# Four changes of order in a local-attention and whitening kernel: a late sum in image 0, an early weight load, band transposes behind a softmax, late bias additions

## The chip, the cores and the metric

The kernel runs on one core of one Trainium2 chip. The time is the device time of one execution in microseconds, and lower is better. Five engines work side by side, each through its own list of instructions in order: PE (TensorE, the matmuls), DVE (VectorE), ACT (ScalarE), POOL (GpSimd) and SP (SyncE, which here only starts DMA transfers). They wait for each other by semaphores.

## What is computed

The input x has 4 images of 256 channels and 64 x 64 points, in fp32. Layer 0 computes, for every point, 49 weights from a 7 x 7 convolution with dilation 2 followed by a 1 x 1 convolution, makes them a softmax, and takes the weighted sum of the 49 neighbours at distance 2. Layer 1 whitens the result: it centres the channels, takes the covariance in 4 groups of 64 channels, finds the inverse root by 5 Newton steps and applies it, with a gain and a shift.

```python
k = conv(x, w1, padding=6, dilation=2) + b1          # 256 -> 128 channels, 7 x 7
k = conv(k, w2) + b2                                 # 128 -> 49, 1 x 1
attn = softmax(k, axis=1)
shifts = [x moved by (2u-6, 2v-6) for u in 0..6 for v in 0..6]
y = sum over k of shifts[k] * attn[k]
Sigma = 1e-5 * I + xc @ xc.T / m                     # xc: y less its mean, per group
P = I; 5 times: P = 1.5 * P - 0.5 * (P @ P @ P) @ (Sigma / trace)
out = (P * sqrt(1 / trace)) @ xc * gain + shift
```

## The kernel before

**Tiles and stages.** The two convolutions are folded into one of 49 outputs. An image is cut into two planes (even and odd rows of the picture); slot tiles hold them. The convolution is a Toom-Cook (Winograd) scheme in rows and columns: seven row points `br` (0 to 5 and `INF`), and under each of them seven column points in three banks (`BANKS`, line 26): points 1, 2, 0, then 3, 4, INF, then 5. For a row point, DVE and ACT combine the rows of x (`row_eval`), then the columns (`col_eval`, into the tiles `xh`), and the tap weights (`weights`, into the tiles `wr`). PE multiplies (`conv_bank`, line 536), ACT brings each bank's sums from PSUM to the tile `pv` (line 546), and DVE turns the points back (`col_interp` into the tile `zz`, then `row_interp` into the logits). `add`, `sub` and `madd` (lines 306, 309 and 313) are the helpers through which nearly all of the DVE arithmetic goes.

**Image 0 is special.** Its row points 0, 4, 5 and INF are convolved directly with the plane (`direct`, line 676), in two sums each for 0, 4 and 5: a first of 8 rows of points, which ACT copies to `zz` (line 688), and a second, whose last row ACT copies (line 690), and whose other rows DVE adds to `zz` (`add` at line 691). The direct sums lie in the PSUM tile `acc` or in a convolution bank. The part of the program for image 0 is run under `strict[0] = True`: `in_turn` chains each `add`, `sub` and `madd` to the one before it, so that DVE executes them in the order in which they are written.

**Images 1 to 3** run through all six of `ROWS` (0 to 5) and `direct_inf`. `conv_step(k, i)` issues bank i of row point k, then prepares bank i of the next row point, and after the last bank turns the columns back. The first time a pair of row point and bank is used, `weights` computes its weights and stores them in DRAM (`gd`, line 434); later images load them (line 378). For row points 4, 5 and INF, the row-combined weights are first read from DRAM (`kept`) into the tile `rb[0]` (line 387), and DVE and POOL read them there. For row point 5 of image 1 this load waits until DVE has read row point 4's weights, since they lie in the same tile.

**Between these steps** lies the attention of the previous image. `softmax` transposes logits with PE, takes maxima with DVE (line 865), exponentials with ACT (line 873) and scales with DVE (line 886). It runs twice for an image (`pc` 0 and 1). `move_terms` copies terms to the tile `zt` with ACT (line 919) and stores them to DRAM (`sd`, line 932); `load_band` reads them back in three parts as diagonals (`band`, line 960, four transfers to a part) and DVE transposes each part in blocks (line 973, under high priority). PE then transposes blocks of x (line 991), multiplies them with the band (`weighted_sum`, line 1020), ACT stores y with the pivot added (line 1039), PE transposes y (line 1052), ACT copies it (line 1060), and PE sums the moments (line 1073). The program's number n counts these units, four to an image: even n use the terms of softmax `pc` 0, odd n those of `pc` 1. The first band is that of n = 0.

**What sets the order.** Outside image 0 a scheduler orders each engine's list by the written order, priorities (`tc.high_priority`) and its own estimates of time; PE's order is written (`pe`). `later` is a list of small ACT steps that `conv_bank` releases behind the ACT copy of the next bank with i = 1: each entry is issued then and made to follow that copy (lines 550 to 560). Before the change only `col_interp`'s last copy (line 633) uses it. `row_interp(b, 0)` for images 1 to 3 is called after row point 4's last bank; it writes the first two of four phases of the logits, and two ACT instructions add the bias to them (line 658, in place). SP's list holds all its transfers in order, and each of them may also wait for the transfer that used the same completion semaphore before it.

Of the kernel before, what the change touches and what calls it, by code (L numbers as in the profile page):

```python
# [10 lines left out]
AF = mybir.ActivationFunctionType  # L11
# [21 lines left out]
def kernel(  # L33
# [330 lines left out]
    def weights(b, br, i, mid=None):  # L364

        first = (br, i) not in made  # L370
        made.add((br, i))
        s0 = slot_of[BANKS[i][0]]
        ns = sum(len(taps(bc)) for bc in BANKS[i])
        nk = NSK * len(taps(br)) // 2
        wt = apool.tile([P, ns, NSK], F32, tag=f"wr{i}", name=f"wr_{b}_{br}_{i}")[:, :, :nk]
        w = {bc: wt[:, slot_of[bc] - s0 : slot_of[bc] - s0 + len(taps(bc))] for bc in BANKS[i]}
        if not first:
            nc.sync.dma_start(wt, gd[br][:, s0 : s0 + ns])
            return w

        if br == 0:
            g = [gr0[:, v] for v in range(KS)]
        elif br in kept:

            f = rb[0].rearrange("p q r c w -> p (q r c w)")[:, : KS * nk]
            if i == 0:
                nc.sync.dma_start(f, kept[br])
            f = f.rearrange("p (v a r k) -> p v a r k", v=KS, a=NCC, k=KT)
            g = [f[:, v] for v in range(KS)]
        else:  # L390
            g = [gbr[:, v] for v in range(KS)]
        g = [t.rearrange("p a r k -> p (a r k)") for t in g]

        e = ct.rearrange("p a b -> p (a b)") if b else store[4].rearrange("p c r w -> p (c r w)")
        e, o, e1 = (e[:, k * nk : (k + 1) * nk] for k in range(3))
        g0 = [g[KS - 1 - a] for a in range(4)]
        g1 = [g[KS - 5 - a] for a in range(3)]
        o0 = {bc: w[bc][:, 0] for bc in w}
        o1 = {bc: w[bc][:, 1] for bc in w if bc != INF}

        same = nc.scalar.copy if b == 0 else nc.gpsimd.tensor_copy
        if i == 0:
            add(e, g0[0], g0[2])
            add(o, g0[1], g0[3])
            add(e1, g1[0], g1[2])
            add(o0[1], e, o)
            sub(o0[2], e, o)
            add(o1[1], e1, g1[1])
            sub(o1[2], e1, g1[1])
            same(o0[0], g0[0])  # L410
            same(o1[0], g1[0])
        elif i == 1:
            madd(e, g0[2], 4.0, g0[0])
            madd(o, g0[3], 4.0, g0[1])
            madd(e1, g1[2], 4.0, g1[0])
            madd(o0[3], o, 2.0, e)
            madd(o0[4], o, -2.0, e)
            madd(o1[3], g1[1], 2.0, e1)
            madd(o1[4], g1[1], -2.0, e1)
            same(o0[INF], g0[3])  # L420
        else:
            madd(o0[5], g0[0], 2.0, g0[1])
            madd(o1[5], g1[0], 4.0, g1[2])
            madd(o0[5], o0[5], 2.0, g0[2])
            if mid is not None:
                mid()
            madd(o1[5], g1[1], 2.0, o1[5])
            madd(o0[5], o0[5], 2.0, g0[3])
            add(o1[5], o1[5], o1[5])
        for bc in BANKS[i]:  # L430
            f = SCALE[bc] * (SCALE[br] if br not in kept else 1.0)
            if f != 1.0:
                nc.scalar.mul(w[bc], w[bc], f)
        nc.sync.dma_start(gd[br][:, s0 : s0 + ns], wt)
        return w
# [205 lines left out]
    def row_interp(b, part):  # L641

        pt = {k: zz[:K2, k] for k in range(NP)}
        lg = lgx
        if b == 0:
            lg = store[4].rearrange("p c r w -> p (c r w)")
        lg = lg[:, : SH * W].rearrange("p (r w) -> p r w", w=W)
        outs = phases(lg[:K2])
        cut = lambda t, k: t[:, k : k + Q8]
        tr = ct.rearrange("p a b -> p (a b)")[:K2, : Q9 * W].rearrange("p (q w) -> p q w", w=W)  # L650
        interpolate(pt, tr, outs, cut, part)
        if part == 0:
            done_ = ((0, outs[0]), (2, outs[2]))
        else:
            done_ = ((3, cut(pt[5], 0)), (1, outs[1]))
            logits[b] = lg
        for a, t in done_:
            nc.scalar.activation(outs[a], t, AF.Identity, bias=bias[:K2])

    logits = {}  # L660

    def direct(b, br, s, ps, w, xr=None):


        a = 3 if br == INF else 0
        order = [(v, cc) for v in sorted(range(KS), key=lambda v: abs(v - R)) for cc in range(NCC)]
        for j, (v, cc) in enumerate(order):
            d = 2 * (v - R)
            w0, w1_ = max(0, -d), min(W, W - d)
            for h in range(2):  # L670
                if xr is None:
                    xs = slots[2 * b + h].rearrange("p c (q a) w -> p a q c w", a=4)[:, a]
                else:
                    xs = xr[:, :, h]
                pe(
                    nc.tensor.matmul(  # L676
                        ps[h * HB : h * HB + KT, :, w0:w1_],
                        w[v][:, cc],
                        xs[:, :, cc, w0 + d : w1_ + d],
                        start=(j == 0),  # L680
                        stop=(j == len(order) - 1),
                        skip_group_check=True,
                    )
                )
        z = zz[:K2, br]
        if s == 0:
            with tc.high_priority():
                nc.scalar.copy(z[:, :Q8], ps[:K2])
        else:
            nc.scalar.copy(z[:, Q8], ps[:K2, Q8 - 1])  # L690
            add(z[:, 1:Q8], z[:, 1:Q8], ps[:K2, : Q8 - 1])

    def conv_psum():
        ncv[0] += 1
# [102 lines left out]
    for i in three:  # L797
        bank(2, i)
    row_weights(4)
    keep_weights(4)  # L800
    xrs[4] = row_eval(0, 4)
    direct0(4, 0)
# [46 lines left out]
    def softmax(b, pc):  # L849

        lv = logits[b].rearrange("p r w -> p (r w)")
        nm = f"{b}_{pc}"
        mx = work.tile([P, NCH, 2], F32, tag="mx", name=f"mx_{nm}")
        lt = []
        for hf in range(2):
            lt.append(tp().rearrange("p (i h k) -> p i h k", i=NI, h=2))
            for i in range(NI):
                pe(
                    nc.tensor.transpose(
                        lt[hf][:, i].rearrange("p h k -> p (h k)")[:, :K2],  # L860
                        lv[:K2, bass.ds(2 * (NI * hf + i) * P + pc, P, 2)],
                        ident[:K2, :K2],
                    )
                )
            nc.vector.tensor_reduce(
                mx[:, NI * hf : NI * (hf + 1)], lt[hf][:, :, :, :KT], AX.X, ALU.max
            )
        nc.vector.tensor_scalar(mx, mx, -1.0, None, ALU.mult)  # L868
        d = terms[b, pc] = bpool.tile([P, 2, NCH, KT], F32, tag="d", name=f"d_{nm}", bufs=2)
        s = work.tile([P, 2, NCH], F32, tag="s", name=f"s_{nm}")  # L870
        for h in range(2):
            for i in range(NCH):
                nc.scalar.activation(  # L873
                    d[:, h, i], lt[i // NI][:, i % NI, h, :KT], AF.Exp,
                    bias=mx[:, i, h : h + 1], accum_out=s[:, h, i : i + 1],
                )
            nc.vector.reciprocal(s[:, h], s[:, h])
            rm = work.tile([P, NCH, KS], F32, tag="rm", name=f"rm_{nm}_{h}")
            nc.vector.tensor_tensor(
                rm,  # L880
                s[:, h].unsqueeze(2).to_broadcast([P, NCH, KS]),
                cmask.unsqueeze(1).to_broadcast([P, NCH, KS]),
                ALU.mult,
            )
            dh = d[:, h].rearrange("p i (u v) -> p i u v", u=KS)
            nc.vector.tensor_tensor(
                dh, dh, rm.unsqueeze(2).to_broadcast([P, NCH, KS, KS]), ALU.mult
            )

    terms, moved, loaded = {}, set(), set()  # L890

# [57 lines left out]

    BAND = ((0, 3), (3, 5), (5, 8))  # L950

    def load_band(n, part):

        if (n, part) in loaded or n not in moved:
# [4 lines left out]
        for g in range(CR):  # L959
# [6 lines left out]
                ),  # L966
            )

        f = band.rearrange("p m r w -> p (m r) w")[
            :, m0 * BP + (R if m0 == 0 else 0) : m1 * BP - (R if m1 == NCH else 0)  # L970
        ].rearrange("p e w -> p (e w)")
        with tc.high_priority():
            nc.vector.transpose(f, f)  # L973
        if (n, part) == (4 * B - 1, len(BAND) - 1):
            bring_back(dma)

# [199 lines left out]

    def soft(b, pc):
        with tc.high_priority() if pc == 0 else nullcontext():
            softmax(b, pc)
        soft_done.add((b, pc))  # L1180
        if pc == 0:
            bands(4 * b)
# [263 lines left out]
```

## Time and profile before

| what | value |
|---|---|
| time, median of 3 runs | 752.98 us (752.46 to 753.97) |
| the profiled execution's own time | 753.07 us |
| its span, first to last instruction | 751.3 us |
| mean granted TensorE clock | 0.984 |
| PE busy | 706.7 us |
| DVE busy | 611.5 us |
| ACT busy | 332.3 us |

A page of the profile shows one execution. "Idle before" an instruction is the time that its engine stood still just before it, with what ended that wait behind an arrow. The timeline view lists instructions as start, length, engine, line, operation and tiles, and puts the idle time and its releaser in square brackets. "Granted clock" is the share of its full clock that PE had. The 1.8 us between the profiled execution's time and its span lie around the program.

### The profile page before, as it was taken

What the parts mean: (1) busy time and instruction counts of PE and PEld (TensorE: products, weight loads), DVE (VectorE), ACT (ScalarE), POOL (GpSimd) and SP (SyncE); (2) the same over time, 40 slices, a digit from 0 to 9 for tenths busy, and PEclk for the clock granted to TensorE, in tenths of its full rate; (3) what the DMA queues carried; (4) which work ended last, traced back from release to release, by engine and by line L of the source; (5) the groups of instructions that cost most, each with busy time, mean ns of one, the idle gap of its engine ahead of it and who ended that gap; (6) DMA issues with size and microseconds to landing.
All of it is one profiled execution on the core that took longest, in us unless ns stands there. A gap on an engine that the chain in (4) does not pass through costs nothing.

```text
span 751.3 us, 18491 instructions
## 1 busy us (share of the span) xinstructions
PE 706.7 (94%) x7512; PEld 531.5 (71%) x7512; DVE 611.5 (81%) x1268; ACT 332.3 (44%) x953; POOL 50.9 (7%) x52
## 2 busy tenths in 40 slices
PE   6999999997988997999999999999999889998996
PEld 1449643376887795599998976899998678885331
DVE  3799899998999988877997799799969665545575
ACT  1424240253564354375453443745435573322564
POOL 0410070020000110001000100000000000000000
PEclk9999999999999998999999999999999999999999
DMA  8981120127153393046743930433532243362588
GB/s 322 257 302 73 60 88 17 64 98 232 64 183 120 103 342 97 21 132 217 256 130 116 336 82 1 146 111 110 166 90 82 50 135 111 117 251 118 209 359 327
DMA packets 59629, 114.41 MB, mean 152 GB/s; under 512 B 22887, under 2 KB 42008, under 8 KB 58776
## 3 DMA queue, kind: packets, MB, share of 16 engines
q1 hardware_dynamic: 55848, 94.36, 37.7%
q0 software_dynamic: 3696, 18.88, 7.3%
q8 instruction: 59, 0.97, 0.5%
q14 instruction: 26, 0.21, 0.1%
HBM read 65.88 MB, written 47.33 MB: 151 GB/s over the span
## 4 chain that ended last, share of the span: by engine, by line
PE 60%; DVE 27%; ACT 5%; DMA 4%; issue 3%; SPq 1%; DVEq 0%; ACTq 0%
PE cv L536 18%; PE y L1020 13%; PE acc L676 6%; PE tp L1386 4%; PE sig L1073 3%; PE tp L1052 3%; PE cv L676 3%; PE tp L991 3%; DVE xh L313 3%; DVE pv L313 2%; DVE rb L313 2%; DVE zz L313 2%; DMA band<-sd 2%; DVE band L973 2%; PE cv L222 2%
## 5 line engine op out<-in xcount | busy, mean ns | idle before, releaser
L536 PE MATMUL cv<-xh,wr 128*49 128x128 f32 x4368 | 249.7, 275 | 5.9 <-DVE xh L306 5.6
L536 PEld LDWEIGHTS cv<-xh,wr 128*49 128x49 f32 x4368 | 243.6, 124 | 9.9 <-issue 7.1
L1020 PE MATMUL y<-band,xb 128*128 128x224 f32 (+2 forms) x640 | 154.6, 381 | 8.7 <-ACT xb L999 6.7
L1020 PEld LDWEIGHTS y<-band,xb 128*128 128x128 f32 x640 | 111.4, 196 | 31.4 <-ACT xb L999 9.4
L546 ACT COPY pv<-cv 113x486 f32<-113x486 f32 (+1 forms) x63 | 30.0, 476 | 84.6 <-PE cv L536 84.4
L1039 ACT ACTIVATE slot<-y,pivot 128x512 f32<-128x512 f32 x53 | 36.7, 740 | 67.5 <-PE y L1020 67.4
L1060 ACT COPY yt<-tp 128x256 f32<-128x256 f32 x128 | 45.5, 379 | 37.8 <-PE tp L1052 36.4
L973 DVE STREAM_TRANSPOSE band<-band 128x864 f32<-128x864 f32 (+1 forms) x48 | 47.6, 992 | 13.2 <-DMA band<-sd 13.1
L991 PE MATMUL tp<-ident,slot 128*128 128x128 f32 x256 | 50.0, 297 | 8.2 <-ACT yt L1060 8.2
L313 DVE SCALAR_TENSOR_TENSOR pv<-pv 113x162 f32<-113x162 f32 x186 | 55.2, 320 | 0.8 <-ACT pv L546 0.3
L1052 PE MATMUL tp<-ident,slot 128*128 128x128 f32 x256 | 52.0, 299 | 3.7 <-ACT yt L1060 1.0
L1052 PEld LDWEIGHTS tp<-ident,slot 128*128 128x128 f32 x256 | 41.2, 205 | 13.8 <-issue 4.0
L991 PEld LDWEIGHTS tp<-ident,slot 128*128 128x128 f32 x256 | 40.1, 205 | 14.8 <-ACT yt L1060 9.7
L873 ACT ACTIVATE d<-tp,mx 128x49 f32<-128x49 f32 x128 | 36.9, 337 | 21.4 <-DVE mx L868 17.9
L919 ACT COPY zt<-d 32x112 f32<-32x112 f32 (+2 forms) x156 | 44.8, 287 | 1.9
L313 DVE SCALAR_TENSOR_TENSOR xh<-ct 128x512 f32<-128x512 f32 x42 | 27.9, 685 | 13.7 <-PE cv L536 13.4
L1073 PEld LDWEIGHTS sig<-yt 128*64 128x64 f32 x1024 | 33.2, 140 | 6.4 <-issue 4.9
L1073 PE MATMUL sig<-yt 128*64 128x65 f32 x1024 | 37.7, 228 | 0.0
L999 ACT COPY xb<-tp 128x256 f32<-128x256 f32 x87 | 30.5, 375 | 14.0 <-PE tp L991 13.4
L999 DVE COPY xb<-tp 128x256 f32<-128x256 f32 x41 | 16.4, 421 | 23.4 <-PE tp L991 23.4
L676 PE MATMUL acc<-slot,tap 128*49 128x496 f32 (+3 forms) x168 | 34.6, 569 | 0.0
L873 ACT ACTIVATION_READ_ACCUMULATOR d<-tp,mx 128x1 f32 x128 | 30.8, 242 | 0.0
(222 smaller groups left out, 958.0 us busy)
## 6 DMA issues: line engine op xcount, KB each, us to landing
out_dram<-out SPq DMA_DIRECT2D x32, 512.0 KB, 3.4
sd<-zt SPq DMA_DIRECT2D x16, 896.0 KB, 4.0
slot<-in_x_dram POOLq DMA_DIRECT2D x12, 1024.0 KB, 10.1
band<-sd SPq DMA_DIRECT2D x128, 84.0 KB, 2.1
wr<-gd SPq DMA_DIRECT2D x15, 588.0 KB, 3.7
wr<-gd SPq DMA_DIRECT2D x15, 490.0 KB, 4.0
spill<-slot POOLq DMA_DIRECT2D x3, 2048.0 KB, 7.7
back<-spill SPq DMA_DIRECT2D x3, 2048.0 KB, 13.1
```

Of the source, the lines that this page charges most:

```text
L313: return in_turn(STT(o, a, f, b, ALU.mult, ALU.add))
L536: nc.tensor.matmul(cv[h * HB : h * HB + KT, k, sr : sr + n, sc : sc + n], wv[:, sc, sr, cc], xh[bc][:, :n, h * NCC + cc, :n], start=(j == ...
L676: nc.tensor.matmul(ps[h * HB : h * HB + KT, :, w0:w1_], w[v][:, cc], xs[:, :, cc, w0 + d : w1_ + d], start=(j == 0), stop=(j == len(order) ...
L873: nc.scalar.activation(d[:, h, i], lt[i // NI][:, i % NI, h, :KT], AF.Exp, bias=mx[:, i, h : h + 1], accum_out=s[:, h, i : i + 1],)
L919: ins = nc.scalar.copy(o, i)
L973: nc.vector.transpose(f, f)
L991: nc.tensor.transpose(t[:, cc * P : (cc + 1) * P], xt[:, cc, CR * m : CR * (m + 1), bass.ds(pc, SW, 2)], ident,)
L999: (nc.vector.tensor_copy if tail else nc.scalar.copy)(xb, t[:, :C])
L1020: nc.tensor.matmul(ps[:, cc, q0 - half * HALF : q1 - half * HALF, :], xb[:, cc * P : (cc + 1) * P], rhs, start=(k == 0), stop=(k == len(PI ...
L1052: nc.tensor.transpose(t[:, cc * P : (cc + 1) * P], yt[:, cc, CR * i : CR * (i + 1), bass.ds(pc, SW, 2)], ident,)
L1060: nc.scalar.copy(yb.rearrange("p a g c -> p (a g) c")[:, :, :GW], t[:, :C].rearrange("p (e c) -> p e c", c=GW),)
L1073: nc.tensor.matmul(sig[g * GW : (g + 1) * GW, cc], yb[:, cc, g, :GW], yb[:, cc, g], start=(count[0] == 0 and cc == 0), stop=(count[0] == 4 ...
```

## The change

The change touches four places.

1. In image 0 the second part of row point 0 (the ACT copy of the last row and the DVE `add` at line 691) is not issued inside `direct`, but put in the list `seconds`, and issued after `row_weights(4)`.
2. For row point 5 the row-combined weights are loaded into `lgx` and not into `rb[0]`. `lgx` is the tile in which the logits of images 1 to 3 are built; in image 1 they are first written after row point 5's weights were computed.
3. The three block transposes of the first band (n = 0) are not issued in `load_band`, but held, and issued after the second softmax of image 0, each made to follow that softmax's last DVE multiplication.
4. The two bias additions of `row_interp(b, 0)` for images 1 to 3 go through `later`, so that they follow the ACT copy of bank 1 of row point 5.

```diff
@@ weights
-            f = rb[0].rearrange("p q r c w -> p (q r c w)")[:, : KS * nk]
+            f = lgx if br == 5 else rb[0].rearrange("p q r c w -> p (q r c w)")
+            f = f[:, : KS * nk]
@@ row_interp
         for a, t in done_:
-            nc.scalar.activation(outs[a], t, AF.Identity, bias=bias[:K2])
+            def end(a=a, t=t):
+                return nc.scalar.activation(outs[a], t, AF.Identity, bias=bias[:K2])
+            if b > 0 and part == 0:
+                later.append(end)
+            else:
+                end()
@@ direct
-            nc.scalar.copy(z[:, Q8], ps[:K2, Q8 - 1])
-            add(z[:, 1:Q8], z[:, 1:Q8], ps[:K2, : Q8 - 1])
+            def second():
+                nc.scalar.copy(z[:, Q8], ps[:K2, Q8 - 1])
+                add(z[:, 1:Q8], z[:, 1:Q8], ps[:K2, : Q8 - 1])
+            if br == 0:
+                seconds.append(second)
+            else:
+                second()
+    seconds = []
@@ image 0
     row_weights(4)
+    seconds.pop()()
     keep_weights(4)
@@ softmax
-            nc.vector.tensor_tensor(
+            last = nc.vector.tensor_tensor(
                 dh, dh, rm.unsqueeze(2).to_broadcast([P, NCH, KS, KS]), ALU.mult
             )
+        return last
+    held = []
+    def release_held(after):
+        for f in held:
+            tc.add_manual_dep(
+                f().ins,
+                after.ins.name,
+                mybir.DependencyInfo(mybir.DependencyClass.NoSync, mybir.DependencyReason.DATA),
+                reason="release_held",
+            )
+        held.clear()
@@ load_band
-        f = band.rearrange("p m r w -> p (m r) w")[
-            :, m0 * BP + (R if m0 == 0 else 0) : m1 * BP - (R if m1 == NCH else 0)
-        ].rearrange("p e w -> p (e w)")
-        with tc.high_priority():
-            nc.vector.transpose(f, f)
+        def turn_blocks():
+            f = band.rearrange("p m r w -> p (m r) w")[
+                :, m0 * BP + (R if m0 == 0 else 0) : m1 * BP - (R if m1 == NCH else 0)
+            ].rearrange("p e w -> p (e w)")
+            with tc.high_priority():
+                return nc.vector.transpose(f, f)
+        if n == 0:
+            held.append(turn_blocks)
+        else:
+            turn_blocks()
@@ soft
         with tc.high_priority() if pc == 0 else nullcontext():
-            softmax(b, pc)
+            last = softmax(b, pc)
+        if pc == 1:
+            release_held(last)
```

## The prediction, as it was put on record

> **What bounds the kernel now.** I read the page's shares, then the list of waits of PE alone, then the timeline around each long wait.
>
> ```profile
> PE 706.7 (94%) x7512; PEld 531.5 (71%) x7512; DVE 611.5 (81%) x1268; ACT 332.3 (44%) x953; POOL 50.9 (7%) x52
> ```
>
> PE is busy for all but 751.3 - 706.7 = 44.6 us of the span. The order of PE's instructions is the same in both builds (I compared their lists), so a gain can come only from PE's idle time and from PE's clock.
>
> ```profile
> PE tp L991 <- ACT yt L1060: 8.2, 8, 3.8
> PE y L1020 <- ACT xb L999: 6.7, 12, 2.2
> PE cv L536 <- DVE xh L306: 5.6, 1, 5.6
> ```
>
> The columns are total, times, longest. A single wait of 5.6 us is on DVE; the ACT waits are traced one step further below. In time order they are (single lines of the timeline, with all others between them left out):
>
> ```profile
> 86.55 0.62 DVE L306 TENSOR_TENSOR zz<-zz,acc 113x448 f32<-113x448 f32 x1 [3.58 <-ACT zz L690]
> 98.78 1.07 PE L676 MATMUL acc<-rb,gbr 128*49 128x512 f32 x4 [0.93 <-DVE rb L313]
> ...
> 183.17 1.08 DVE L973 STREAM_TRANSPOSE band<-band 128x864 f32<-128x864 f32 x1 [2.82 <-DMA band<-sd]
> 184.25 0.37 SPq L378 DMA_DIRECT2D wr<-gd  x1
> 188.72 0.46 PE L536 MATMUL cv<-xh,wr 128*49 128x128 f32 x2 [5.59 <-DVE xh L306]
> ...
> 208.28 0.69 ACT L486 COPY xh<-rb 128x512 f32<-128x512 f32 x1 [2.98 <-DVE rb L313]
> 212.49 0.39 PE L991 MATMUL tp<-ident,slot 128*128 128x128 f32 x1 [1.79 <-ACT yt L1060]
> 234.83 0.53 ACT L433 ACTIVATE wr<-wr 128x392 f32<-128x392 f32 x1 [2.48 <-DVE wr L306]
> 236.09 0.50 PE L1020 MATMUL y<-band,xb 128*128 128x96 f32 x1 [2.18 <-ACT xb L999]
> 241.94 0.36 DVE L313 SCALAR_TENSOR_TENSOR wr<-rb 128x196 f32<-128x196 f32 x1 [0.53 <-PE cv L536]
> 252.78 0.53 ACT L433 ACTIVATE wr<-wr 128x392 f32<-128x392 f32 x1 [4.38 <-DVE wr L306]
> 256.10 0.54 PE L1020 MATMUL y<-band,xb 128*128 128x320 f32 x1 [1.23 <-ACT xb L999]
> 286.34 1.08 DVE L973 STREAM_TRANSPOSE band<-band 128x864 f32<-128x864 f32 x1 [2.90 <-DMA band<-sd]
> 288.02 0.72 ACT L658 ACTIVATE lgx<-lgx,bias 113x512 f32<-113x512 f32 x1 [3.38 <-DVE lgx L306]
> 290.20 0.38 PE L991 MATMUL tp<-ident,slot 128*128 128x128 f32 x1 [3.76 <-ACT yt L1060]
> ```
>
> Call PE's waits A (188.7), B (212.5), C (236.1), D (256.1) and E (290.2). In B, C and D ACT stands behind an instruction that waits for DVE (L486 on rb, L433 on wr), and PE's block copy is queued behind that on ACT. So from 180 to 262 us DVE sets the pace, through ACT, although PE is the busiest engine: in that stretch DVE has almost no idle time except the 2.82 us at 183.17. How early DVE is there decides the gain.
>
> PE's clock is a second loss. The view of chosen stretches gives, in columns, length, busy time (count) of PE, PEld, DVE, ACT and POOL, granted clock, DMA share and GB/s:
>
> ```profile
> 188.40:191.70 3.30, 2.98 (x28) 3.02 (x30) 3.30 (x7) 3.30 (x23) 0.00 (x0) 0.50 0.28 105
> 236.20:239.50 3.30, 3.30 (x38) 3.01 (x39) 3.30 (x11) 1.36 (x2) 0.00 (x0) 0.50 0.68 235
> 256.70:260.00 3.30, 3.30 (x7) 2.02 (x6) 3.30 (x14) 0.00 (x0) 0.00 (x0) 0.50 0.35 96
> 290.80:297.50 6.70, 6.15 (x14) 3.83 (x12) 6.70 (x17) 1.58 (x5) 0.00 (x0) 0.50 0.00 0
> ```
>
> After A, C and D PE runs at half clock for 3.4 us, after E for 6.8 us. Half a clock for 3.4 us loses 1.7 us.
>
> **What the Trainium skill says.** "TensorE: Matmul & The Clock Gate", Part 1: the clock falls to half after an idle window of about 3.4 us, windows run freely, and a busy window restores it. The trace agrees: stretches of 3.4 us at 0.50. Part 4 of that page: transposes through PE do not count as busy in the same way. The trace fits: D has only 1.23 + 0.29 us of idle time in its window, but transposes lie between, and it is followed by half clock; B, with 1.79 us, isn't. The same page, architectural detail of Part 1: ACT and DVE are strict first-in-first-out; B, C and D are this. "DMA: Bandwidth & Descriptors", Queues, rings and completion order: each DMA engine takes a ring's descriptors in order. The trace agrees, see A.
>
> **Part 1, the late sum.** It removes a DVE wait of 3.58 us before the `add` at 86.55. The two instructions (ACT copy 0.21 us, DVE add 0.62 us, 0.54 from start to start) are neither removed nor doubled. DVE goes on from 82.97 with the column sums that stood behind the add (87.09 before, so 4.12 sooner), and has row point 4's weights at 96.35 - 4.12 = 92.2. The add after that needs PE's sum of 86.1, long done, and the row combination that PE waits for (96.35 to 98.6) ends by 95.0. Neither issues a transfer. ACT scales gbr (L326, 97.02 before) at about 93.0 to 94.4. PE is ready at 97.85, so its 0.93 us disappear. DVE is then 3.6 us ahead, but at 122.92 it waits for PE's second sum of row point 4 (already 0.85 us before), so all that remains behind that is PE's lead of 0.93. Hidden cost: zero; cover is 2.8 us (95.0 against 97.85).
>
> **Part 3, the held transposes.** DVE no longer stands 2.82 us at 183.17, and the three transposes (1.00 + 0.76 + 1.00 us from start to start) follow the second softmax. On DVE behind the old wait stood the maximum's sign change (185.76), so ACT's exponentials (185.96, after 8.1 us without work), the column sums of the next row point and its `xh`. Without the wait DVE, 0.93 + 2.82 = 3.75 us ahead, passes the last scaling at about 188.6 and ends the transposes at 191.4. PE needs them for the first weighted sum (196.68 before, about 195.3 now): 3.9 us of cover. New waits: DVE's reciprocals wait for ACT's exponentials. Started at 181.3 and taking 5.15 us with the two PSUM copies between (185.96 to 191.06 before), they end at 186.5, DVE comes at 186.8; I take 0, bounds 0 and 1.
>
> What follows A? `xh` would be ready at about 184, 4.6 us sooner. But the weights of this bank are loaded behind the twelve band loads on SP, at 184.25, and a load of 588 KB takes 3.7 us to land by the page: 187.95. The packets (4,704 bytes each) ran from 185.25 to 188.19, behind the last band packets (to 185.36). So a transfer takes the place of the wait on DVE: A shrinks by only 188.72 - 188.29 = 0.43 us, plus 0.93, with which the whole chain of transfers moves, since its start (ACT's copies to zt) moves. PE's lead after A: 1.36. Bounds: 0.9 and 5.5 (if the load isn't needed so soon). It matters little, because B and C are decided by DVE.
>
> B: DVE's rb comes 3.75 sooner, ACT's queue up to the yt copy takes 3.8 us (208.28 to 212.07), so yt is at 208.4 to 208.7; PE comes at 210.70 - 1.36 = 209.3. B is gone: PE's lead is 1.36 + 1.79 = 3.15. C: PE would come at 233.91 - 3.15 = 230.8, the copy behind L433 at 236.05 - 3.75 = 232.3: 1.6 us of wait instead of 2.18, and PE's lead is 3.75. With 1.6 us of idle time the window holds more work (3.4 - 1.6 = 1.8 us) than B's did (3.4 - 1.8 = 1.6 at most), so I expect no half clock there: 1.7 us that PE gains at once. Most of that is lost again: D is DVE's too (ACT's 4.38 us). What DVE gets from it is its own wait on PE at 241.94, 0.53 us. So the lead at D's end is 3.75 + 0.53 = 4.28 us, D itself is about 2.2 us, and half clock after it stays.
>
> **Part 2, the other tile.** The load of 686 KB moves from 244.62 to about 156, behind DVE's last reading of lgx (156.1), before the store of wr and the next load (163.40): 7 us of cover on SP, and the queue must not be late before about 167, as PE needs that next load at 171.12. At 245 it was landed at 248.5 by its packets (5,488 bytes), DVE used it at 250.43 with no wait. So nothing is removed from the path: 0. Bounds: -0.5 (DVE comes 0.5 us closer to an old landing) and +0.5.
>
> **Part 4, the bias.** In the instruction lists both additions now stand behind the PSUM copy of bank 1 (284.10), but still before bank 2's copy and before yt. ACT's wait of 3.38 us on DVE's `lgx` stays ahead of the yt copy, DVE's there is on a band transfer (286.34) which PE's own progress at 276 starts. E stays at 3.76. Value 0; bounds -0.7 (one addition's length) and +0.6.
>
> **Sum.** 0.93 + 2.82 + 0.53 = 4.28; 753.07 - 4.28 = 748.79. I take 748.8. After E everything moves as a whole. The profiled execution is 0.09 us above the median, which I neglect.
>
> **Rivals.**
> - *DVE's lead is lost on the way* (a band, ACT or exponential wait takes its place): only part 1 and the 0.43 us at A reach the end, 753.07 - 1.36 = 751.7. For: DVE's list has many waits that end just before they matter; at 145.89 its slack is 0.26 us. Against: the band packets of n = 1 end at 223.0 and row point 4's load at 228.1 with DVE coming later to both.
> - *The clock at D recovers too*: 1.7 us more, 747.1. For: D's window fell just so; windows run freely. Against: its idle time grows.
> - *Slower: the transposes, now tied to the softmax, come late for PE's first weighted sum.* If ACT's exponentials do not start sooner, the last scaling ends at 193.5 as before and the transposes at 197.4, 2.1 us after PE is there (195.3), with half clock of 1.7 us, while B, C and D stay: 753.07 - 1.36 + 3.8 = 755.5. It decides from 195.3 on. Against: nothing but the transposes holds the sign change (its maxima are done at 179.4).
> - *Nothing moves*, because other waits refill each gap: 753.
>
> **How the numbers follow.** The forecast 0.56 (own range 747.9 to 750.0), lost lead 0.15, clock at D 0.16, slower 0.07, nothing 0.06. The range 746.6 to 751.9 leaves out the slower case, nothing, and tails of the rest. A measurement can tell about 0.2% (1.5 us) from no change. Faster by more: forecast, clock case and a quarter of the lost lead, 0.76; same: the rest of it and nothing, 0.17; slower 0.07.
>
> **What would show it.** Right: no DVE wait before the add; PE's wait at 97.85 gone; A still about 5 us, with the DMA as releaser; B gone; C 1.6 and D 2.2 us; E unchanged. Wrong: A under 3 us, a PE wait on band at the first weighted sum, or E changed by over 1 us.

## The result and the profile after

| | before | after |
|---|---|---|
| first measurement, median | 751.81 us (6 runs) | 746.24 us (6 runs, 745.64 to 755.14) |
| its ratio, 95% interval | | 0.9942 [0.9917, 0.9966] |
| measured again with three variants (e5) | 752.92 us (14 runs) | 747.80 us (6 runs, 746.69 to 750.82) |
| its ratio, 95% interval | | 0.9927 [0.9899, 0.9955] |
| profiled execution | 753.07 us, span 751.3 | 746.19 us, span 744.4 |

The change makes the kernel 0.6 to 0.7% faster by the two ratios. In microseconds the two medians lie 1.0 and 2.6 us under the forecast of 748.8, and the first of them 0.36 us under its range (746.6 to 751.9). But the forecast was taken from one execution of 753.07 us, and the kernel before took 751.81 us in the first measurement. Taken as a gain, 4.28 us were forecast, and 4.4 (0.58% of 751.81) and 5.5 us (0.73% of 752.92) are measured by the ratios, 5.6 and 5.1 us by the medians. All parts of the profile below are of the first measurement's profiled execution. Shares of the page:

```profile
PE 703.4 (94%) x7512; PEld 528.3 (71%) x7512; DVE 611.3 (82%) x1268; ACT 332.5 (45%) x953; POOL 51.6 (7%) x52
```

The work of DVE and ACT is the same to 0.2 us. PE is busy 3.3 us less with the same 7,512 matmuls. Most of that is its clock: PE is busy for 19.5 us at half clock before and for 14.1 us after, which makes 2.7 us. Its idle time is 41.0 instead of 44.6 us. PE's waits, with total, times and longest:

```profile
PE tp L1032 <- ACT yt L1101: 6.7, 7, 3.5
PE y L1061 <- ACT xb L1040: 5.9, 13, 1.3
PE cv L538 <- DVE rm L899: 5.3, 1, 5.3
```

In time order (timeline, lines between left out; the waits are A at 187.59, B at 210.87, C at 232.59, D at 249.66 and 251.67, E at 283.83):

```profile
122.02 0.62 DVE L306 TENSOR_TENSOR zz<-zz,acc 113x448 f32<-113x448 f32 x1 [1.93 <-ACT zz L701]
...
183.62 1.33 SPq L378 DMA_DIRECT2D wr<-gd  x3
187.59 7.52 PE L538 MATMUL cv<-xh,wr 128*49 128x128 f32 x96 [5.31 <-DVE rm L899]
...
210.87 3.18 PE L1061 MATMUL y<-band,xb 128*128 128x320 f32 x12 [0.31 <-ACT xb L1040]
231.32 0.95 ACT L435 ACTIVATE wr<-wr 128x392 f32<-128x392 f32 x2 [1.62 <-DVE wr L306]
232.59 0.69 PE L1061 MATMUL y<-band,xb 128*128 128x96 f32 x4 [1.32 <-ACT xb L1040]
248.35 0.53 ACT L435 ACTIVATE wr<-wr 128x392 f32<-128x392 f32 x1 [4.91 <-DVE wr L306]
249.66 0.51 PE L1032 MATMUL tp<-ident,slot 128*128 128x128 f32 x2 [0.81 <-ACT yt L1101]
251.67 3.18 PE L1061 MATMUL y<-band,xb 128*128 128x320 f32 x12 [1.24 <-ACT xb L1040]
281.65 0.72 ACT L662 ACTIVATE lgx<-lgx,bias 113x512 f32<-113x512 f32 x1 [3.45 <-DVE lgx L306]
283.83 0.70 PE L1032 MATMUL tp<-ident,slot 128*128 128x128 f32 x2 [3.52 <-ACT yt L1101]
```

DVE waits neither at the moved add nor at the band transposes, which now run in one piece of 2.75 us from 188.55 on and end 4.7 us ahead of PE's first weighted sum (191.3 against 196.04). It now waits longer at 122.02 for the sum of row point 4. B's long wait is gone; 0.31 us is left one instruction later. In C and D the chain is still ACT behind DVE's `wr`. The granted clock in the stretches where before had half clock (columns as before: behind the length and the five engines comes the clock):

```profile
185.00:191.70 6.70, 4.11 (x40) 4.14 (x42) 6.70 (x13) 2.18 (x13) 0.00 (x0) 0.50 0.50 191
236.20:239.50 3.30, 3.30 (x64) 3.30 (x62) 3.30 (x8) 1.13 (x3) 0.00 (x0) 1.00 0.42 152
252.00:255.40 3.40, 3.40 (x32) 2.52 (x32) 3.40 (x15) 0.51 (x1) 0.00 (x0) 1.00 0.44 125
284.00:287.30 3.30, 3.03 (x8) 2.04 (x9) 3.30 (x10) 2.00 (x6) 0.00 (x0) 0.50 0.00 0
```

The half clock is gone after C and after D, and lasts one stretch instead of two after E (from 287.40 to 294.00 the clock is 1.00).

**Where the time came from.** PE's list is the same in both kernels, so PE's lead can be read at any instruction: its start in the trace of before less its start in the trace of after. It is 1.12 us after A, 2.64 after B, 3.51 at C, 4.42 at D's end; then 6.11 behind the stretch after D that runs at full clock, 6.37 at E's end, 8.29 behind E's stretch; it stays so through images 2 and 3, and 1.4 us are lost in the whitening, where after has two stretches of half clock (from 679.9 and from 690.1) and before has one (from 686.7). 753.07 - 6.88 = 746.19, which is the profiled time.

### The profile page after: what moved, and what is told of

Its sections match the earlier page's. It is cut to its first block, busy times and chain, and to the rows that moved or that the text cites. A ratio compares the mean times of both kernels' runs of the same rounds, so it can differ in the third digit from the quotient of the medians.

```text
span 744.4 us, 18491 instructions
## 1 busy us (share of the span) xinstructions
PE 703.4 (94%) x7512; PEld 528.3 (71%) x7512; DVE 611.3 (82%) x1268; ACT 332.5 (45%) x953; POOL 51.6 (7%) x52
## 4 chain that ended last, share of the span: by engine, by line
PE 61%; DVE 28%; ACT 4%; issue 3%; DMA 2%; SPq 0%; DVEq 0%; ACTq 0%
PE cv L538 20%; PE y L1061 12%; PE acc L685 6%; PE tp L1429 4%; PE tp L1093 3%; PE sig L1114 3%; PE cv L685 3%; PE tp L1032 3%; DVE xh L313 3%; DVE pv L313 3%; DVE zz L313 2%; DVE rb L313 2%; PE cv L222 2%; DVE ct L313 2%; DVE band L1009 2%
## 5 line engine op out<-in xcount | busy, mean ns | idle before, releaser
L1061 PE MATMUL y<-band,xb 128*128 128x224 f32 (+2 forms) x640 | 150.6, 373 | 7.6 <-ACT xb L1040 5.9
L1061 PEld LDWEIGHTS y<-band,xb 128*128 128x128 f32 x640 | 109.1, 192 | 29.0 <-ACT xb L1040 8.9
L313 DVE SCALAR_TENSOR_TENSOR xh<-ct 128x512 f32<-128x512 f32 x42 | 27.8, 683 | 14.1 <-PE cv L538 13.7
```

Of the source, the lines that this page charges most:

```text
L313: return in_turn(STT(o, a, f, b, ALU.mult, ALU.add))
L1061: nc.tensor.matmul(ps[:, cc, q0 - half * HALF : q1 - half * HALF, :], xb[:, cc * P : (cc + 1) * P], rhs, start=(k == 0), stop=(k == len(PI ...
```

## The experiments

Each kernel was timed in 6 to 22 runs beside the kernel before on the same chip. The lead is read as above, in us, from one profile each:

| kernel | median | ratio to before [95%] | after A | after B | at C | D's end | after D's stretch |
|---|---|---|---|---|---|---|---|
| forecast | 748.8 | | 1.36 | 3.15 | 3.75 | 4.28 | 4.28 |
| e1 part 1 | 751.06 | 0.9981 [0.9961, 1.0000] | 0.46 | 0.47 | 0.09 | 0.37 | 2.06 |
| e2 part 3 | 749.91 | 0.9986 [0.9964, 1.0008] | -0.23 | 1.56 | 2.41 | 3.32 | 5.01 |
| e3 parts 1, 3 | 748.84 | 0.9960 [0.9942, 0.9978] | 1.12 | 2.93 | 3.78 | 4.68 | 6.37 |
| e4 parts 2, 4 | 752.35 | 1.0007 [0.9985, 1.0029] | 0.53 | 0.50 | 0.32 | 1.23 | 1.23 |
| e5 all four | 747.80 | 0.9927 [0.9899, 0.9955] | 1.55 | 3.73 | 4.19 | 5.11 | 5.11 |
| e6 parts 1, 2, 3 | 747.78 | 0.9921 [0.9895, 0.9946] | 0.91 | 2.31 | 3.66 | 4.57 | 6.27 |
| e7 parts 1, 3, 4 | 748.58 | 0.9933 [0.9908, 0.9958] | 1.51 | 3.50 | 3.77 | 4.68 | 4.68 |
| e8 additions written late | 748.45 | 0.9944 [0.9916, 0.9972] | 0.63 | 1.28 | 3.37 | 4.28 | 4.28 |
| e9 additions late | 747.23 | 0.9928 [0.9903, 0.9954] | 1.63 | 2.90 | 3.76 | 4.69 | 6.38 |
| e10 scaling late | 745.95 | 0.9926 [0.9892, 0.9959] | -3.30 | -1.55 | 0.80 | 3.88 | 5.57 |
| e11 both late | 744.42 | 0.9893 [0.9857, 0.9929] | | | | | |
| e12 early load | 753.66 | 1.0006 [0.9991, 1.0021] | 3.99 | 5.79 | 8.14 | 4.08 | 3.46 |

**e1, e2, e3, e4: one part or two alone.** Each is the changed kernel with hunks undone; the four undoings are

```diff
 part 1 undone, in direct (and no seconds.pop()() after row_weights(4))
+            second()
 part 2 undone, in weights
+            f = rb[0].rearrange("p q r c w -> p (q r c w)")
 part 3 undone, in load_band
+        turn_blocks()
 part 4 undone, in row_interp
+            end()
```

> The kernel before with part 1 alone (the late second sum of row point 0). Theory 'DVE's lead, part by part': PE's wait of 0.93 us at 97.85 disappears and nothing behind it changes, so 0.9 us less than the kernel before (ratio 0.9988), plus or minus one half-clock stretch of 1.7 us if a window falls otherwise; the waits A to E stay at about 5.6, 1.8, 2.2, 1.5 and 3.8 us, and DVE still stands 2.8 us at the first band transpose. Rival 'part 1 is absorbed': at 122.92 and at the first band transpose DVE waits anyway, 0.0 us. Rival 'the whole lead counts': 3.6 us less, as much as DVE gains at the add.

> The kernel before with part 3 alone (the band transposes of n = 0 held behind the second softmax). Theory: DVE's 2.8 us at the first band transpose go; A shrinks by under 1 us because the weight load behind the bands takes its place; B disappears or keeps under 0.4 us; C shrinks by about half a microsecond; 2.8 to 3.4 us less than the kernel before (ratio 0.9955 to 0.9963), and 1.7 us more for each of the half-clock stretches after C and D that goes. Rival 'a band or exponential wait refills it': 0.4 us less. Rival 'A is DVE's and shrinks fully': A 2.8 us or less.

> Parts 1 and 3 without the other tile (part 2) and without the late bias (part 4). Theory: the same as the changed kernel with all four, within 0.5 us (746.2; ratio to before 0.994), with E at 3.5 to 3.8 us. Rival 'the early load or the late bias carries the surplus of the result over the forecast' (2.6 us more than forecast): 748.8, with the wait on row point 4's weights or E larger by 0.5 to 2 us.

> Parts 2 and 4 without parts 1 and 3. Theory: no difference from the kernel before within 0.5 us (ratio 1.000), plus or minus one half-clock stretch (1.7 us, 0.2%); DVE's waits before the add (3.6 us) and at the first band transpose (2.8 us) are both there, A to E as before. Rival 'parts 2 and 4 bring something by themselves': 0.5 to 2.5 us less, seen at E or at 244 to 252 us.

Part 1 alone gives 1.1 us by the medians (its interval just reaches no change), but at C the lead is only 0.09 us; the rest in its trace is D's stretch at full clock. So the expected 0.9 us were met by another route than the expected one. DVE's gain is given back twice (timeline of e1):

```profile
121.68 0.62 DVE L306 TENSOR_TENSOR zz<-zz,acc 113x448 f32<-113x448 f32 x1 [3.25 <-ACT zz L698]
182.71 1.08 DVE L1006 STREAM_TRANSPOSE band<-band 128x864 f32<-128x864 f32 x1 [3.66 <-DMA band<-sd]
```

At 121.68 it waits 3.25 us for PE's sum, as forecast. At the band it waits 3.66 instead of 2.82 us: ACT's copies to `zt` began 1.2 us sooner, and SP issued the last load of this part 1.20 us sooner (at 175.58 instead of 176.78), but the load landed only 0.46 us sooner (at 182.53 instead of 182.99). What held it under way wasn't shown. Part 3 alone gives 2.3 us by the medians; its ratio stays unclear, since 16 of its 22 runs lie at 746.9 to 752.9 and 6 at 754.8 to 757.3. None of those six was profiled, and what lengthens them stays open. Parts 1 and 3 together have the lead of all four, and more than their sum at C (3.78 against 0.09 + 2.41): without part 3 DVE stands at the band, and part 1's lead ends there. In time, though, e3 stood at 748.84, the number that the rival in its expectation names, and not at 746.2; the larger wait that the rival asks for isn't there (E is 3.00 us). Parts 2 and 4 alone change nothing that these runs can tell. The rivals "parts 2 and 4 bring something" and "the whole lead counts" fall. In e3 the profile also names A's releaser (the timeline of PE):

```profile
187.60 4.66 PE L538 MATMUL cv<-xh,wr 128*49 128x128 f32 x50 [5.62 <-DMA wr<-gd]
```

The load's last packet ended at 187.11, and PE started 0.49 us later. In every profile with part 3 and this order of loads in which I measured it (after, e2, e3, e5 to e9) the distance is 0.46 to 0.50 us, also where the page names DVE.

**e5, e6, e7: all four again, without part 4, without part 2.** The edits are undoings from the list above; e5 has none.

> The changed kernel again, in more runs and on one chip with the next three. In the runs so far it stood at 746.2 (6 runs) and parts 1 and 3 alone at 748.8 (22 runs), while parts 2 and 4 alone gave +0.2. Theory 'parts 2 and 4 are worth nothing': the median of more runs is about that of parts 1 and 3, 748 to 749, and the six runs of the first measurement were a lucky draw of half-clock stretches. Rival 'parts 2 or 4 act only together with 1 and 3': it stays at 746 to 747.

> Parts 1, 2 and 3, without the late bias. Theory: the same as all four within 0.7 us, with E's wait 0 to 0.5 us shorter than with part 4, since the first addition is done before the copy of bank 1 and DVE's band arrives no earlier. Rival 'part 4 carries 2 us': 2 us more than all four.

> Parts 1, 3 and 4, without the other tile for row point 5's weights. Theory: the same as all four within 0.5 us; the load at about 238 lands before DVE needs it. Rival 'part 2 is cover for the lead that parts 1 and 3 give' (DVE comes 5 us closer to the old landing): a DVE wait of 0.5 to 2 us on that load between 240 and 247, and 1 to 2 us more than all four at D.

e5's 747.80 lies between what its two expectations name. The three medians lie within 0.8 us, with overlapping runs: neither part 2 nor part 4 is worth anything that these runs can tell while the other is there. Both undone together were timed only in e3, on another chip; its ratio is 0.0033 above e5's, with overlapping intervals, and its profile has no less lead than those of all four. E was 2.93 us without the late bias and 2.55 and 3.83 with it; in all profiles with the old order of ACT at E it is 2.5 to 4.1 us and follows the landing of the band, which PE's progress starts. No wait of DVE on the load of part 2 shows up when it stays in `rb[0]` (e7).

e5 is the same program as after, with the same two waits at D (0.81 us at 248.97 and 1.24 us at 250.99), and yet half clock follows (the view of chosen stretches):

```profile
251.50:254.70 3.20, 3.20 (x8) 2.03 (x7) 3.20 (x15) 0.00 (x0) 0.00 (x0) 0.50 0.38 110
```

So whether D costs 1.7 us more isn't set by the length of the waits, but by where they fall in the clock's windows, from run to run. Within each trace the half-clock stretches start whole multiples of 3.413 us apart (to 3 ns), and this gives the edges of the windows between them. In e5 both waits of D lie in one window (first line, then the window behind it); in after an edge at 249.80 parts them:

```profile
247.98:251.39 3.41, 1.36 (x8) 0.91 (x7) 3.41 (x7) 3.23 (x10) 0.00 (x0) 1.00 0.34 126
251.39:254.80 3.41, 3.41 (x8) 2.24 (x7) 3.41 (x15) 0.00 (x0) 0.00 (x0) 0.50 0.39 118
```

```profile
246.39:249.80 3.41, 2.60 (x23) 2.22 (x18) 3.38 (x10) 1.45 (x5) 1.31 (x1) 1.00 0.10 24
249.80:253.22 3.42, 2.18 (x10) 1.60 (x11) 3.42 (x11) 2.10 (x7) 0.00 (x0) 1.00 0.58 202
253.22:256.63 3.41, 3.41 (x46) 2.83 (x44) 3.41 (x14) 1.73 (x4) 0.07 (x1) 1.00 0.26 66
```

PE stands for 2.05 us of the window in e5, and for 0.81 and 1.24 us of the two in after. The other profiles agree: 2.04 and 2.05 us in one window in e7 and e8, which have the half clock; at most 1.46, 1.23 and 1.22 us in one window in e3, e6 and e9, which don't. At C the same: 2.18 us in one window in before, and half clock; 2.37 us in e4, parted into 1.77 and 0.60, and none.

**e8 and e9: what holds E.** Two tries at moving image 1's first two bias additions behind the second half's first addition. The edit of e9, against the changed kernel:

```diff
-            if b > 0 and part == 0:
-                later.append(end)
+            if b == 1 and part == 0:
+                biases.append(end)
+            elif b > 0 and part == 0:
+                later.append(end)
             else:
-                end()
+                last = end()
+        if part == 1:
+            while biases: # each made to follow `last`
```

> The changed kernel, but in image 1 the two bias additions follow the first bias addition of the other half of the logits, some 14 us later, so that ACT no longer stands at E behind DVE's sums of the logits, which stand behind the band transfer. Theory 'E is ACT behind DVE behind the band': E falls from 3.5 us to under 0.5 us and the half clock after E goes, 3.2 to 5 us less than all four (741 to 743 if all four are at 746). Rival 'E is PE's own cycle through PSUM and the copies': E stays above 2.5 us. Rival 'the wait moves': E goes but a PE wait of 2 to 3 us comes at the next block transposes.

The kernel of e8 held the additions back in the written order only (`biases.pop(0)()`, for all three images) without the dependency on `last`, and the scheduler put them where before had them. So it tested nothing about E: it stands as one more kernel without part 4, with E at 3.79.

> The changed kernel, with the two bias additions of image 1's first half of the logits made to follow the first bias addition of the second half, some 14 us later, by a dependency (the run before had them only written later). No other engine's list changes. Theory 'E is ACT behind DVE behind the band': E falls from 2.6 to 3.8 us to under 0.6 us, the half clock after E (1.7 us) mostly goes, and nothing is late next, since PE's waits behind E are all under 0.7 us: 3 to 5 us less than the changed kernel, 743 to 745. Rival 'the wait moves': E goes, but PE waits 2 to 3 us in one of the next four block copies because ACT then reaches DVE's later sums; 747 to 748. Rival 'E is the cycle through PSUM': E stays above 2.5 us.

With the dependency E is gone: PE starts there at 279.89 without a wait (0.45 us are left just behind it, at 280.98), and its lead goes from 6.38 to 10.31 there and to 13.57 at the instruction that before runs at 298 us. E was ACT standing behind DVE behind the band. But the ratio to the kernel before is that of e5 (0.9928 and 0.9927). In its trace the lead falls to 7.35 by a new wait in the next block copies but one (timeline of e9):

```profile
310.93 0.30 ACT L906 ACTIVATE d<-tp,mx 128x49 f32<-128x49 f32 x1 [4.66 <-DVE mx L901]
...
320.67 0.50 PE L1045 MATMUL tp<-ident,slot 128*128 128x128 f32 x2 [1.85 <-ACT yt L1114]
```

ACT waits for DVE's maxima, then works without a gap through 16 exponentials, a PSUM copy and eleven copies to `zt` (3.28 us from 315.92 on); the block copy that PE needs is queued behind them. PE waits 1.85 + 0.61 us, and 6.8 us of half clock follow. Theory and "the wait moves" were both right, for different parts.

**e10 and e11: what holds C and D.** ACT's scaling of two banks' weights is held and made to follow a block copy (e10, against the changed kernel; e11 has this and the edit of e9).

```diff
+        if (b, br, i) in ((1, 4, 0), (1, 5, 0)):
+            scales.append(scale)      # the nc.scalar.mul lines and the store to gd
+        else:
+            scale()
...
-        make_block(n, 4)
+        scale_behind(make_block(n, 4))
...
-        turn_y(n, 3)
+        scale_behind(turn_y(n, 3))
```

> The changed kernel, with ACT's scaling of the weights of row points 4 and 5, bank 0, in image 1, made to follow the block copy that PE waits for at C and the fourth yt copy at D. Theory 'C and D are ACT standing behind DVE's weights with PE's block copies queued behind it': C (1.3 to 1.9 us) and D (0.8 + 1.2 us) fall under 0.6 us each, while DVE's own list is nearly unchanged: 2 to 4 us less at D's end. But DVE still sets the pace of the banks, so PE may wait for xh or wr at the start of the banks that follow instead (rival 'DVE itself, not ACT's order': 0 to 1 us less, with a new wait on xh or wr at 234 to 237 or at 257 to 260).

C and D are gone: from 215.06 to 269 PE has no wait of over 0.3 us, and between A and D's end it gains 7.2 us (-3.30 to 3.88), where e5 gains 3.6. No wait on `xh` or `wr` came in their place. So part of C and D was ACT's order, not DVE's pace. One wait of the same kind is new, at a bank's scaling that the edit leaves alone (e10, ACT and PE):

```profile
269.40 0.53 ACT L437 ACTIVATE wr<-wr 128x392 f32<-128x392 f32 x1 [3.25 <-DVE wr L306]
270.71 1.34 PE L1085 MATMUL y<-band,xb 128*128 128x320 f32 x4 [1.33 <-ACT xb L1063]
```

The profile of e10 was one of three runs at 750 to 752 (the other four took 744.9 to 746.0): DVE stood 7.75 us for a transfer of x in image 0, which the edit doesn't touch, and PE was 3.3 us late from 100 us on. The lead of e10 is to be read with that:

```profile
46.87 2.36 DVE L306 TENSOR_TENSOR rb<-slot 128x1024 f32<-128x1024 f32 x2 [7.75 <-DMA slot<-in_x_dram]
```

A late PE could by itself make waits on other engines vanish. But DVE is as late as PE here: its last sum of C's weights (L309) starts at 231.21 in after and at 235.44 in e10, 4.23 us later, and PE comes 4.20 us later behind B. So the lateness doesn't explain that C and D are gone. In the medians the gain is not clear: e10's ratio (0.9926) is that of e5.

> Both together. Theory: the gains add, since they lie at different places, 5 to 8 us less than the changed kernel (739.5 to 743). Rival: what is won at C and D comes back at E or in the banks behind it, because DVE is then later against PE: no better than the late bias alone.

Median 744.42; 7 of 9 runs lie at 742.7 to 744.9. It has the lowest median of the study, 1.1% under before, about 2.8 us under e9 and 1.5 us under e10 of the same series (the intervals of the three ratios overlap): less than the 5 to 8 us under the changed kernel that I expected. One of its executions, the one that was profiled, took 1413 us with PE busy for 1392 of them; why isn't known. It is left out of the comparison, so no trace of this kernel is read, and where the rest went wasn't shown.

**e12: the load that ends A.**

```diff
-            nc.sync.dma_start(wt, gd[br][:, s0 : s0 + ns])
+            with tc.high_priority() if (b, br, i) == (1, 2, 0) else nullcontext():
+                nc.sync.dma_start(wt, gd[br][:, s0 : s0 + ns])
```

> The changed kernel, with the weight load that ends A (row point 2, bank 0, image 1) placed on SP's list behind the first four of the twelve band loads instead of behind all twelve. The scheduler also places some sums of DVE and some copies of ACT behind that point differently, so the time tells less than the trace. Theory 'A is the transfer, but its size hardly matters, since DVE decides C and D': A falls from 5.3 to between 1 and 2.5 us, PE's lead over the kernel before is then 3.5 to 5.5 us after A, and at D's end it is what it was, 4 to 5 us, with C that much longer; the time is that of the changed kernel (746 to 748.5). Rival 'A counts': the 3 to 4 us stay to the end, 743 to 745. Rival 'A is not the transfer': A stays above 4.5 us.

```profile
184.73 7.17 PE L539 MATMUL cv<-xh,wr 128*49 128x128 f32 x96 [2.82 <-DMA wr<-gd]
243.28 1.08 DVE L1010 STREAM_TRANSPOSE band<-band 128x864 f32<-128x864 f32 x1 [6.55 <-DMA band<-sd]
252.02 5.49 PE L1062 MATMUL y<-band,xb 128*128 128x320 f32 x12 [5.97 <-ACT xb L1041]
287.90 3.38 PE L539 MATMUL cv<-xh,wr 128*49 128x128 f32 x32 [8.80 <-DVE xh L313]
```

A falls to 2.82 us, so it was the transfer. Against the theory, the gain did not stop at C: the lead is 8.14 there. It is lost at D and E. At D the scheduler's new order puts a band transpose so early that DVE stands 6.55 us at it and PE waits 5.97 us; PE's 8.80 us at E come behind two more waits of DVE (2.54 and 2.89 us) and were not taken apart further. D's is the very pattern that part 3 takes away at 183 us. The time is that of the kernel before, not the 746 to 748.5 us expected. Since DVE's and ACT's order changed too, it isn't shown what an early load is worth in the changed kernel's own order.

## Why the prediction was right, step by step

- **What bounds the kernel** (DVE's lead, through ACT, from 180 to 262 us): right in its main point. The seven profiles with parts 1 and 3 differ by 2.45 us in lead after B (1.28 to 3.73) and by 0.82 at C (3.37 to 4.19): what PE has before is levelled where it waits for DVE's chain (e8, the last of them, has no wait at C). It needs a correction: e10 shows that C and D could go with DVE's work as it was, so the pace came from ACT's order as much as from DVE.
- **Part 1**: the 0.93 us at 97.85 are gone, and DVE's surplus is absorbed at 122 us, as written. That this 0.93 reaches the end by itself, as the rival "lead lost" assumes, is wrong: e1 has 0.09 us of it at C. In company with part 3 it counts: e3 is 1.37 us ahead of e2 at C.
- **Part 3**: the 2.82 us are gone, the transposes take 2.75 us and hinder nobody, and no wait of DVE on the exponentials shows (bounds 0 and 1, value 0). That the load takes DVE's place at A was right, but not the 0.43 us: in before the load's last packet ended at 188.19, and with the 0.46 to 0.50 us that PE comes behind it, the load alone would have let PE start at 188.65 to 188.69, hardly before the 188.72 at which DVE let it start. Part 3 alone leaves A at 5.69 us (e2). In after A is 5.31 instead of 5.59 us because the load itself ended 1.06 us sooner and PE came 0.84 us sooner. The rival on late transposes has a slip too: 193.5 and 2.76 us make 196.3, not 197.4.
- **B, C, D**: forecast gone, 1.6 and 2.2 us; measured 0.31, 1.32 and 2.05 us (0.81 + 1.24). DVE's wait of 0.53 us at 241.94 is gone, as the sum needs. Lead at D's end: forecast 4.28, measured 4.42 in after and 4.28 to 5.11 in the six other profiles. That 4.42 comes so near is in part luck: the lead at C was 3.51 and not 3.75, and from C to D's end 0.91 us came and not 0.53.
- **Clock**: no half clock after C was right in all seven. The term that was mis-sized is "half clock after D stays". It stayed in three of seven profiles (e5, e7, e8) and went in four (after, e3, e6, e9), 1.7 us each; the rival that gave this 0.16 and 747.1 us describes the first measurement's profile as far as D's end and its stretch, and the forecast should have taken it as an even chance. An estimate from the traces says the same: at D half clock followed where 1.52 us or more of waits fell into one window (1.52 in before, 1.84 in e4, 2.04 and 2.05 in e5, e7 and e8) and not where at most 1.46 us did (e3; less in the others). Waits of 0.81 and 1.24 us with 0.78 us between them leave 1.5 us or more in one window for 1.68 of the 3.41 us at which an edge can lie, which is 0.49. "TensorE: Matmul & The Clock Gate", Part 1 of the Trainium skill, which I used, says that the windows run freely, 3.4 us long (the stretches here are 3.41 us); e5 beside after shows what that means: one program, the same 0.81 and 1.24 us, and both outcomes. "After E everything moves as a whole" left out that stretches come and go also at E (one instead of two, 1.9 us with the shorter waits) and in the whitening (-1.4 us).
- **What falls into a window**: the forecast compared whole waits, not what falls into one window. Its B, "1.79 us" without half clock, is parted by an edge at 212.26: PE is busy for 1.85 us of the window before it, and for 1.89 us of D's window, which was followed by half clock. So a window with B leaves at least 1.6 us of work, not at most. That transposes between the waits weigh in, as the forecast says, fits the traces: 1.52 us of waits with 1.19 us of transposes were followed by half clock (before at D), 1.56 us with 0.83 us (B) and 1.77 us with 0.39 us (e4 at C) were not. No run tests it alone.
- **Part 2 and part 4**: forecast 0 and 0, and e4, e6, e7 agree within what they can tell. The load of part 2 moved to 155.27, as written. E was forecast unchanged: 3.76 to 3.52.

## What to carry to other kernels

Look for the instruction at which the pace-setting engine stands for a transfer while it has other work in its list, and hold that instruction until the transfer is surely there. Then ask the same of the engine between it and PE: moving two of ACT's scalings behind PE's copies removed C and D (e10), and moving two additions removed E (e9), though a later wait took that gain back. In time, both together (e11) stand 2.6 us lower than e5 by the ratios, with overlapping intervals. Leads add only where no wait between them levels them, so cost parts together at the next shared wait. Where waits of 1 to 4 us decide, count the clock's half-speed stretches separately and as chances, by how much of the waits can fall into one window.

## What was unexpected

- Half clock came in stretches of 3.41 us, which began at the same place in one run and not in another of the same program (after and e5 at D), with an edge of the clock's windows as the difference. One stretch costs 1.7 us, more than the forecast's bounds for part 2 (0.5 us) or part 4 (0.7 us).
- A long wait does not cost its clock in proportion: after A's 5.3 us, two stretches follow in after (184.95 to 191.78, the first mostly inside the wait, 2.64 of 3.41 us) and one in e5 (186.54 to 189.95).
- An input transfer of image 0 was late enough in one profiled run to hold DVE 7.75 us (e10), which put PE 3.3 us behind; the same transfer held DVE 2.23 us in after and 1.79 us in e5.
